# A first batch loaded in parts, unread products in idle stretches, earlier table and statistics, stores in sixteen parts

## The chip, the cores and the metric

The kernel runs on one core of a Trainium2 chip. The metric is the device time of one execution in microseconds; lower is better. A core has five engines that run side by side, each in its own order: TensorE (PE, matrix products), VectorE (DVE), ScalarE (ACT), GpSimd (POOL) and SyncE (SP, which here only issues transfers). They wait for each other by semaphores. Transfers can be issued from SP's, ACT's and POOL's queues.

## What is computed

The input is x with shape (4, 128, 64, 64): four batches of 4096 tokens with 128 channels, in float32. Two layers are run, cut here to what matters.

```python
# layer 0: attention over all 4096 positions of a batch, 64 channels
q, k, v = wq @ xf, wk @ xf, wv @ xf              # xf: (b, 128, 4096)
att = softmax(k^T q, axis=2)                     # (b, 4096, 4096)
x = x + wo @ (att v)
# layer 1
t = tokens(x)                                    # (b, 4096, 128)
t = t + causal_attention(layernorm(t))           # q, k, v by 128x128 weights
wx = batchnorm(layernorm(t) @ W^T)               # mean and variance over all 4*4096 rows
y_0 = 0;  y_s = sigmoid(wx_s + V y_(s-1))        # along the 4096 tokens
out = t + y
```

The batch statistics need every block of every batch, so the recurrence can't begin before the last one.

## The kernel before, in words

All of it is in `fast_path`. A second path, `general_path`, follows in a branch that is taken only if a flag computed at the end asks for it; in the profile it is not taken.

**Opening (L398 to L469, L806 to L821).** The weights are loaded from ACT's queue with `load`, the input from SP's queue in 16 transfers of 512 KB, all four batches one after the other (L410 to L412). PE's first product is `g_ps` (L468), which forms the matrix g1 from wqT and wkT. Then, for batch 0, the function `keys(0, m)` is run for m = 0 to 3, all ahead of the attention: `cols0` makes a block of keys and queries (two products kr_ps, L490, copied by DVE and ACT) and sends half of each copy to other partitions with a transfer (`swap`, L496); `vals0` makes the values (v_ps, L502), and `vals0_by_tokens` transposes them (vT_ps, L512).

**Attention (L693 to L849).** The work of both layers is a list of items. An item scores two tiles of 128 keys against 512 queries (`scores`: s_ps by PE at L704 or L713, an exponential on ACT at L718 or L720); two items later `values` adds up acc on PE (L764 or L772); `sums` adds the exponentials on DVE (L744). Layer 0 takes 16 items for each block of 512 queries; there are eight blocks to a batch. One loop over slots `s` writes this out by hand. In each slot one further piece of work may go in: either one that is due (a block's normalisation, its projection, its LayerNorm) or the next of a list called `side`, which holds the `keys` of the next batch while layer 1 of the present one runs:

```python
            if due:
                w = min(due, key=lambda w: w[0])
                waiting.remove(w)
                w[1]()
                push(s, w[2])
            elif side:
                side.pop(0)()
```

`rows` prepares the queries two blocks ahead, and in layer 0 calls `tokens0`, which overwrites a block of the input in `xs` with the same block laid out by tokens (a transfer from xT, L526).

**A block's end in layer 1 (`finish1`, L618).** Three steps: `first` divides and adds to the residual (`project`), stores the result to x2 and normalises it (`normed`, with a power on POOL at L450); `second` transposes it; `third` multiplies with W (wx_ps, L653), takes batch statistics with bn_stats (L656) into `stats`, and ACT copies wx back into `xs` (L660, L662). For the last block of all (`final`) the transposition is done on PE, as nothing is left to hide a slower way.

**Recurrence and output (L856 to L949).** After the last block, DVE aggregates the 32 statistics (`bn_aggr`, L868), a chain of small operations makes scale and shift, and the recurrence starts. It cuts each batch into 256 chunks that run side by side, 12 warming steps and 16 kept ones, four batches in turn: a product (y_ps, L907), one DVE operation (L909), a sigmoid (L912; the very first at L904). `residual` then transposes the states on PE, adds them on DVE to the residual read back from x2 (L927), and stores each half of a batch, 1 MB, once its 16 steps are done (L928).

The order of instructions on each engine is not wholly the source's: independent instructions may change places when the program is built.

Of the kernel before, what the change touches and what calls it, by code (L numbers as in the profile page):

```python
# [15 lines left out]
P = 128  # L16
# [333 lines left out]
def fast_path(  # L350
# [44 lines left out]

    x2 = dram.tile([B, N, P], F32, name="x2")

    def load(name, shape, *parts):  # L398
        t = const.tile(shape, F32, name=name)
        for dst, src in parts:  # L400
            nc.scalar.dma_start(out=dst(t), in_=src)
# [5 lines left out]
    wqk = load("wqk", [P, P], (lo, c_wqT), (hi, c_wkT))  # L407
    wkq = load("wkq", [P, P], (lo, c_wkT), (hi, c_wqT))
    wv0 = load("wv0", [P, M], (whole, c_wvT))
    for b in range(B):  # L410
        for g in range(N // CHUNK):
            nc.sync.dma_start(out=xs[:, b, ts(g, CHUNK)], in_=x[b, :, ts(g, CHUNK)])  # L412
    wo2 = load("wo2", [P, P], (top, c_woT), (bottom, c_woT))
    wqT = load("wqT", [P, P], (whole, a_wqT))
    wkT = load("wkT", [P, P], (whole, a_wkT))
    wv1 = load("wv1", [P, P], (whole, a_wv))
    wf = load("wf", [P, P], (whole, f_wT))
    vf = load("vf", [P, P], (whole, f_vT))
    gamma = load("gamma", [P, 1], (whole, f_gamma))
    beta = load("beta", [P, 1], (whole, f_beta))  # L420

    ident = const.tile([P, P], F32, name="ident")
    make_identity(nc, ident)
# [16 lines left out]
    quarter = const.tile([P, TPB, Q], F32, name="quarter")  # L440
    for j in range(TPB):
        nc.vector.tensor_reduce(quarter[:, j], ident.rearrange("p (q r) -> p q r", r=S), AX.X, ALU.add)
    good = const.tile([P, 1], F32, name="good")
    g1 = const.tile([P, P], F32, name="g1")
    recs = const.tile([P, 2, B, NT], F32, name="recs")
    stats = const.tile([P, B * NB, nc.vector.BN_STATS_DIM], F32, name="stats")

    def rsqrt(y, var, z):

# [6 lines left out]
    with tc.tile_pool(name="batch", bufs=1) as batch, tc.tile_pool(name="rows", bufs=2) as rowp, tc.tile_pool(  # L456
# [7 lines left out]
        def misc(name):  # L464
            return ps_m.tile([P, BLK], F32, tag="m", name=name)

        gp = misc("g_ps")
        nc.tensor.matmul(gp[:, :P], lhsT=wqT, rhs=wkT, start=True, stop=True)  # L468
        nc.vector.tensor_copy(g1, gp[:, :P])  # L469

        class Batch:
            pass
# [121 lines left out]
        def in_range():  # L594
# [5 lines left out]
            nc.vector.tensor_tensor(r, r, r2, ALU.mult)  # L600
            nc.vector.tensor_reduce(good, r, AX.X, ALU.add)

        def finish0(b, g):

            agg, den = bs[b].agg, bs[b].den

            def norm():
                if g == 0:
                    bs[b].xh = batch.tile([P, NT, P], F32, tag="xh", name="xh")
                    bs[b].xhT = batch.tile([P, N], F32, tag="xhT", name="xhT")  # L610
                normed(b, g, bs[b].xh[:, ts(g, TPB)])

            yield 2, lambda: (project(0, b, g, agg, den), norm())
            fill.append(
                lambda: transposed(bs[b].xh[:, ts(g, TPB)], bs[b].xhT[:, ts(g, BLK)], "xhT_ps", nc.scalar.copy)
            )

        def finish1(b, g):  # L618
            agg, den = bs[b].agg, bs[b].den
            mem = {}  # L620
            final = b == B - 1 and g == NB - 1

            def first():
                project(1, b, g, agg, den)
                nc.sync.dma_start(
                    out=x2[b, ts(g, BLK)].rearrange("(j p) c -> p j c", p=P),
                    in_=xs[:, b, ts(g, BLK)].rearrange("p (j c) -> p j c", c=P),
                )
                mem["xh"] = wk.tile([P, TPB, P], F32, tag="xh2", name="xh2")
                normed(b, g, mem["xh"])  # L630

            def second():
                mem["xhT"] = wk.tile([P, BLK], F32, tag="xhT2", name="xhT2")
                if final:
                    transposed(mem["xh"], mem["xhT"], "xh2T_ps", nc.vector.tensor_copy)
# [13 lines left out]
                nc.sync.dma_start(out=mem["xhT"], in_=by_c.rearrange("c r q k -> (c r) (q k)"))  # L649

            def third():
                wp = misc("wx_ps")
                nc.tensor.matmul(wp, lhsT=wf, rhs=mem["xhT"], start=True, stop=True)  # L653
# [12 lines left out]

            yield 1, first
            yield 3, second
            yield 1 if final else 4, third
# [133 lines left out]
                lambda: vals0_by_tokens(b, m, mem[0]),  # L803
            ]

        for m in range(NB // 2):  # L806
            for task in keys(0, m):
                task()
        SKEW = 2
        side = []  # L810

        def rows():

            if blocks:
                layer, b, g = blocks.pop(0)
                (rows1 if layer else rows0)(b, g)
                if layer == 0:
                    tokens0(b, g)

        rows()  # L820
        rows()  # L821
        for s in range(len(items) + SKEW + 16):
# [8 lines left out]
            if 0 <= s - SKEW < len(items):  # L831
                it = items[s - SKEW]
                values(it)
                if it.last:
                    rows()
                    if fill:
                        fill.pop(0)()
                    push(s, (finish1 if it.layer else finish0)(it.b, it.g))
# [7 lines left out]
                push(s, w[2])  # L846
            elif side:
                side.pop(0)()
        assert not waiting and not side and not fill  # L849


# [4 lines left out]
    with tc.tile_pool(name="xr", bufs=1) as xrp, tc.tile_pool(name="y", bufs=2) as yp, tc.tile_pool(  # L856
# [11 lines left out]
        nc.vector.bn_aggr(mv, stats)  # L868
# [50 lines left out]
        def residual(b):  # L919

            for h in range(HALVES):
                for s0 in range(0, STEPS, TPB):
                    ps = ps_r.tile([P, TPB, P], F32, tag="r", name="yT_ps")
# [86 lines left out]
```

## Time and profile before

| | |
|---|---|
| Time, three runs | 2142.74, 2143.60 (median), 2145.57 us |
| Profiled execution | timed at 2148.17 us, span 2146.4 us |
| PE busy | 2097.3 us (98%) |
| Weight loads of PE (overlap with it) | 922.9 us (43%) |
| DVE, ACT, POOL busy | 1466.3 (68%), 1008.5 (47%), 104.1 us (5%) |
| DMA | 64.99 MB, mean 30 GB/s |

A busy PE means that a product was under way by the records, whose ends are modelled; it does not mean that the array was at its peak. The page also gives the TensorE clock that was granted, in tenths of full speed, for 40 slices of the span. A timeline row has its start, how long it took, engine, line, operation, output and inputs; "x8" merges eight instructions, and the bracket tells how long the engine stood idle before it and what released it. Rows with a small q (SPq, ACTq) issue transfers. All shares are means over stages with different limits, so stages are read one by one.

### The profile page before, as it was taken

To read this page: it belongs to the slowest core of one execution; us is meant where nothing else is said; L and a number is where in the kernel's file an instruction comes from. 1 tells how busy PE (TensorE), PEld (TensorE's weight loads), DVE (VectorE), ACT (ScalarE), POOL (GpSimd) and SP (SyncE) were. 2 spreads that over 40 slices of the span, in tenths; PEclk is the share of its full clock that TensorE was granted. 3 is DMA by queue.
4 is the path that set the end of the run, shared out by engine and by line. 5 is a ranking of instruction groups with operands and counts; after the bars stand their busy time and mean duration, and the time that the engine had idled before them with its cause. 6 is when DMAs were issued, how large, how long until landed. Compare 5 with 4: busy or idle time off the path is not lost. (4 is left out here: it accounts for less than half of the span.)

```text
span 2146.4 us, 30417 instructions
## 1 busy us (share of the span) xinstructions
PE 2097.3 (98%) x12016; PEld 922.9 (43%) x12016; DVE 1466.3 (68%) x2807; ACT 1008.5 (47%) x1098; POOL 104.1 (5%) x207
## 2 busy tenths in 40 slices
PE   6999999999999999999999999999999999999978
PEld 2333344444333344444333334444433334544446
DVE  3788875454788876554588887545478887754478
ACT  3666633323566643333466663332356664323355
POOL 0000010000000000000000001000000001000000
PEclk9999999999999999999999999999999999999989
DMA  7000022000000002110000002200000000110043
GB/s 226 1 1 2 1 60 54 20 15 15 16 2 1 2 6 74 40 30 15 16 1 1 2 1 59 59 16 15 15 16 1 1 2 6 40 30 15 15 162 159
DMA packets 65319, 64.99 MB, mean 30 GB/s; under 512 B 5648, under 2 KB 55056, under 8 KB 63120
## 3 DMA queue, kind: packets, MB, share of 16 engines
q1 hardware_dynamic: 63280, 62.41, 9.7%
q8 instruction: 96, 1.57, 0.3%
q10 hardware_dynamic: 1888, 0.56, 0.1%
q14 instruction: 55, 0.45, 0.1%
HBM read 33.85 MB, written 24.90 MB: 27 GB/s over the span
## 5 line engine op out<-in xcount | busy, mean ns | idle before, releaser
L744 DVE TENSOR_TENSOR dsum<-dsum,p 128x1024 f32<-128x1024 f32 x676 | 826.8, 1223 | 451.6 <-ACT p L720 320.6
L718 ACT ACTIVATE p<-s_ps,nshift 128x1024 f32<-128x1024 f32 x512 | 571.2, 1116 | 356.7 <-PE s_ps L704 337.7
L720 ACT ACTIVATE p<-s_ps 128x1024 f32<-128x1024 f32 (+2 forms) x288 | 274.2, 952 | 564.2 <-PE s_ps L713 542.5
L764 PE MATMUL acc<-p,v 64*64 64x512 f32 x4096 | 533.8, 592 | 1.7 <-ACT half L783 1.7
L704 PE MATMUL s_ps<-swap,kr 64*64 64x512 f32 x2048 | 533.0, 598 | 2.5 <-DMA swap<-kr 2.5
L704 PE MATMUL s_ps<-kr 64*64 64x512 f32 x2048 | 533.0, 598 | 0.0
L713 PE MATMUL s_ps<-rows,xhT 128*128 128x512 f32 (+3 forms) x1152 | 503.1, 559 | 1.4 <-DVE rows L535 1.4
L772 PE MATMUL acc<-p,xh 128*128 128x512 f32 (+3 forms) x1152 | 501.5, 557 | 0.0
L772 PEld LDWEIGHTS acc<-p,xh 128*128 128x128 f32 x1152 | 215.6, 190 | 241.3 <-issue 231.8
L713 PEld LDWEIGHTS s_ps<-rows,xhT 128*128 128x128 f32 x1152 | 212.9, 190 | 242.3 <-issue 196.4
L764 PEld LDWEIGHTS acc<-p,v 64*64 64x64 f32 x4096 | 155.1, 134 | 288.0 <-issue 269.0
L704 PEld LDWEIGHTS s_ps<-swap,kr 64*64 64x64 f32 x2048 | 137.9, 134 | 138.3 <-issue 129.1
L704 PEld LDWEIGHTS s_ps<-kr 64*64 64x64 f32 x2048 | 137.9, 134 | 128.3 <-issue 123.7
L450 POOL TENSOR_TENSOR ln_rstd<-ln_var,mhalf 128x4 f32<-128x4 f32 x64 | 65.7, 1027 | 1211.3 <-DVE ln_var L579 1200.5
L752 DVE TENSOR_TENSOR dsum<-dsum,p 128x256 f32<-128x256 f32 (+1 forms) x120 | 55.7, 498 | 74.3 <-POOL p L724 74.3
L567 DVE SCALAR_TENSOR_TENSOR xs<-o_ps,recs,xs 128x128 f32<-128x128 f32 x256 | 72.3, 343 | 8.7 <-PE o_ps L562 3.1
L583 DVE TENSOR_SCALAR xh<-xs,ln_mv,ln_rstd 128x128 f32<-128x128 f32 x256 | 71.3, 342 | 2.2
L724 POOL TENSOR_SCALAR_AFFINE_SELECT p<-p 128x128 f32<-128x128 f32 x128 | 34.4, 292 | 665.6 <-ACT p L720 650.7
L742 DVE COPY dsum<-p 128x1024 f32<-128x1024 f32 x60 | 41.3, 689 | 35.3 <-ACT p L720 26.6
L576 DVE BATCH_NORM_STATS2 ln_st<-xs 128x6 f32<-128x128 f32 x256 | 63.4, 269 | 0.0
L662 ACT COPY xs<-wx_ps 128x512 f32<-128x512 f32 x31 | 18.1, 585 | 83.6 <-DVE stats L656 76.7
L909 DVE SCALAR_TENSOR_TENSOR z<-xs,scale,y_ps 128x256 f32<-128x256 f32 x108 | 48.5, 480 | 5.7 <-PE y_ps L907 4.4
(115 smaller groups left out, 1043.5 us busy)
## 6 DMA issues: line engine op xcount, KB each, us to landing
xs<-in_x SPq DMA_DIRECT2D x16, 512.0 KB, 8.8
xs<-in_xT SPq DMA_DIRECT2D x32, 256.0 KB, 3.2
x<-xs SPq DMA_DIRECT2D x32, 256.0 KB, 2.3
xr<-x SPq DMA_DIRECT2D x8, 1024.0 KB, 12.3
out_x<-xr SPq DMA_DIRECT2D x8, 1024.0 KB, 6.0
by_c<-sqT SPq DMA_DIRECT2D x124, 64.0 KB, 1.8
xhT<-by_c SPq DMA_DIRECT2D x31, 256.0 KB, 2.7
swap<-kr SPq DMA_DIRECT2D x32, 128.0 KB, 2.2
```

The lines of the kernel that those rows point to most:

```text
L450: nc.gpsimd.tensor_tensor(y, var, mhalf[:, : y.shape[-1]], ALU.pow)
L567: nc.vector.scalar_tensor_tensor(t, in0=op[:, ts(j, P)], scalar=rec[:, j : j + 1], in1=t, op0=ALU.mult, op1=ALU.add)
L576: nc.vector.bn_stats(st[:, j], xs[:, b, ds(g * BLK + j * P, P)])
L583: nc.vector.tensor_scalar(dst[:, j], xs[:, b, ds(g * BLK + j * P, P)], mv[:, j, 0:1], y[:, j : j + 1], ALU.subtract, ALU.mult)
L704: nc.tensor.matmul(ps[c * M : c * M + M, off : off + n], lhsT=bs[it.b].kr[part, h, ds(t % (NT // 2) * P + c * M, M)], rhs=rows[h], start=True,
L713: nc.tensor.matmul(ps[:, off : off + n], lhsT=lhsT, rhs=rhs, start=True, stop=True)
L718: nc.scalar.activation(it.p[:, :off], ps[:, :off], AF.Exp, bias=nshift)
L720: nc.scalar.activation(it.p[:, :off], ps[:, :off], AF.Exp, scale=float(P) ** -0.5)
L744: nc.vector.tensor_tensor(flat, flat, it.p, ALU.add)
L752: nc.vector.tensor_tensor(den[:, h, q0:], den[:, h, q0:], it.p[:, o : o + n], ALU.add)
L764: nc.tensor.matmul(bt.acc[h * M : h * M + M, r], lhsT=bt.v[part, t], rhs=it.p[part, o : o + n], start=it.first, stop=it.last,)
L772: nc.tensor.matmul(bt.acc[:, 0, q0:], lhsT=bt.xh[:, t], rhs=it.p[:, o : o + n], start=it.first and h == 0, stop=it.last and h == 1,)
```

## The change

1. Input: of the input only batch 0 is loaded at the start, in eight transfers of 256 KB, in the order of blocks 0, 4, 1, 5, 2, 6, 3, 7. The next batch is loaded in four transfers of 512 KB while block 0 of the present one ends; a small copy on POOL, which writes into the place to be loaded, makes these transfers wait.
2. Weights: those that the first products don't need go to POOL's queue: wo2, wqT, wkT and wv1 at the start, the others in `load_rest`.
3. `keys(0, m)`: part 0 and the first step of part 1 run ahead of the attention. The rest of part 1, parts 2 and 3, and `form` (g_ps) go to `side`. `tokens0` of the first two blocks is called once `side` is empty.
4. Unread products: twelve of 128 columns before the first keys; in the last block nine, one and six of 256 columns. Their results are not read.
5. Statistics: `ahead` aggregates 31 blocks before the last one and packs count, mean and variance times count into `ends`; the last aggregation has 9 numbers in place of 192.
6. Table: in the last block one sigmoid of one column, read by nobody, stands ahead of `project`.
7. Stores: each half of a batch is stored in two parts of eight steps.

The diff, cut to its core:

```diff
-    for b in range(B):
-        for g in range(N // CHUNK):
-            nc.sync.dma_start(out=xs[:, b, ts(g, CHUNK)], in_=x[b, :, ts(g, CHUNK)])
+    for m in range(NB // 2):
+        for g in (m, m + NB // 2):
+            nc.sync.dma_start(out=xs[:, 0, ts(g, BLK)], in_=x[0, :, ts(g, BLK)])
...
+    wo2 = load(nc.gpsimd, "wo2", [P, P], (top, c_woT), (bottom, c_woT))
+    wqT = load(nc.gpsimd, "wqT", [P, P], (whole, a_wqT))
+    wkT = load(nc.gpsimd, "wkT", [P, P], (whole, a_wkT))
+    wv1 = load(nc.gpsimd, "wv1", [P, P], (whole, a_wv))
...
+    stats = const.tile([P, B * NB - 1, nc.vector.BN_STATS_DIM], F32, name="stats")
+    ends = const.tile([P, 9], F32, name="ends")
+    nc.gpsimd.memset(ends[:, 0:1], float((B * NB - 1) * BLK))
+    spare = const.tile([P, 1], F32, name="spare")
...
+        wp = misc("warm_ps")
+        for _ in range(12):
+            nc.tensor.matmul(wp[:, :P], lhsT=ident, rhs=ident, start=True, stop=True)
+
+        def form():
+            gp = misc("g_ps")
+            nc.tensor.matmul(gp[:, :P], lhsT=wqT, rhs=wkT, start=True, stop=True)
+            nc.vector.tensor_copy(g1, gp[:, :P])
+
+        def load_rest():
+            for t, src in ((wf, f_wT), (vf, f_vT), (gamma, f_gamma), (beta, f_beta)):
+                nc.gpsimd.dma_start(out=t, in_=src)
...
+        def ahead():
+            mv = stat.tile([P, nc.vector.BN_AGGR_DIM], F32, tag="mv1", name="mv1")
+            nc.vector.bn_aggr(mv, stats)
+            nc.vector.tensor_copy(ends[:, 1:2], mv[:, 0:1])
+            nc.vector.tensor_tensor(ends[:, 2:3], mv[:, 1:2], ends[:, 0:1], ALU.mult)
...
             def first():
+                if final:
+                    nc.scalar.activation(spare, agg[:, 0:1], AF.Sigmoid)
                 project(1, b, g, agg, den)
+                if final:
+                    warm(9, agg[:, : BLK // 2])
...
                     transposed(mem["xh"], mem["xhT"], "xh2T_ps", nc.vector.tensor_copy)
+                    warm(1, mem["xh"][:, 2:])
...
-                nc.vector.bn_stats(stats[:, b * NB + g], wp)
+                nc.vector.bn_stats(ends[:, 3:] if final else stats[:, b * NB + g], wp)
+                if b == B - 1 and g == NB - 2:
+                    ahead()
...
                     nc.scalar.copy(to.rearrange("p (s c) -> p s c", c=CPB), wp.rearrange("p (c s) -> p s c", s=STEPS))
+                    warm(6, to[:, : BLK // 2])
...
-        for m in range(NB // 2):
-            for task in keys(0, m):
-                task()
+        parts = [keys(0, m) for m in range(NB // 2)]
+        for task in parts[0][:2] + parts[1][:1] + parts[0][2:]:
+            task()
         SKEW = 2
-        side = []
+        side = parts[1][1:] + parts[2] + parts[3] + [form]
...
+        def tokens():
+            while started:
+                b, g = started.pop(0)
+                tokens0(b, g)
+                if g == 2 and b + 1 < B:
+                    nc.gpsimd.tensor_copy(
+                        xs[:, b + 1].rearrange("p (k n) -> p k n", n=CHUNK)[:, :, 0], bs[b].agg[:, : N // CHUNK]
+                    )
+                    for k in range(N // CHUNK):
+                        nc.sync.dma_start(out=xs[:, b + 1, ts(k, CHUNK)], in_=x[b + 1, :, ts(k, CHUNK)])
...
             elif side:
                 side.pop(0)()
+                if not side and items[s].b == 0 and items[s].layer == 0:
+                    tokens()
+                    load_rest()
...
-        nc.vector.bn_aggr(mv, stats)
+        nc.vector.bn_aggr(mv, ends)
...
-                nc.sync.dma_start(out=by_chunk(out)[b, h], in_=xr[:, b, h])
+                    if s0 % (2 * TPB):
+                        nc.sync.dma_start(out=by_chunk(out)[b, h, :, part], in_=xr[:, b, h, part])
```

More of the change, by code (lines that the diff above doesn't have):

```diff
@@ L396, in fast_path, with load @@
     x2 = dram.tile([B, N, P], F32, name="x2")
-    def load(name, shape, *parts):
+    def load(engine, name, shape, *parts):
         t = const.tile(shape, F32, name=name)
         for dst, src in parts:
-            nc.scalar.dma_start(out=dst(t), in_=src)
+            engine.dma_start(out=dst(t), in_=src)
         return t
@@ L406, in fast_path @@
     top, bottom = (lambda t: t[0:M]), (lambda t: t[M:P])
-    wqk = load("wqk", [P, P], (lo, c_wqT), (hi, c_wkT))
-    wkq = load("wkq", [P, P], (lo, c_wkT), (hi, c_wqT))
-    wv0 = load("wv0", [P, M], (whole, c_wvT))
-    for b in range(B):
-        for g in range(N // CHUNK):
[L412 to L420, printed above, removed]
+    wqk = load(nc.scalar, "wqk", [P, P], (lo, c_wqT), (hi, c_wkT))
+    wkq = load(nc.scalar, "wkq", [P, P], (lo, c_wkT), (hi, c_wqT))
+    wv0 = load(nc.scalar, "wv0", [P, M], (whole, c_wvT))
+    for m in range(NB // 2):
+        for g in (m, m + NB // 2):
+            nc.sync.dma_start(out=xs[:, 0, ts(g, BLK)], in_=x[0, :, ts(g, BLK)])
     ident = const.tile([P, P], F32, name="ident")
@@ L442, in fast_path @@
         nc.vector.tensor_reduce(quarter[:, j], ident.rearrange("p (q r) -> p q r", r=S), AX.X, ALU.add)
+    wf = const.tile([P, P], F32, name="wf")
+    vf = const.tile([P, P], F32, name="vf")
+    gamma = const.tile([P, 1], F32, name="gamma")
+    beta = const.tile([P, 1], F32, name="beta")
+    wo2 = load(nc.gpsimd, "wo2", [P, P], (top, c_woT), (bottom, c_woT))
+    wqT = load(nc.gpsimd, "wqT", [P, P], (whole, a_wqT))
+    wkT = load(nc.gpsimd, "wkT", [P, P], (whole, a_wkT))
+    wv1 = load(nc.gpsimd, "wv1", [P, P], (whole, a_wv))
     good = const.tile([P, 1], F32, name="good")
@@ L445, in fast_path @@
     recs = const.tile([P, 2, B, NT], F32, name="recs")
-    stats = const.tile([P, B * NB, nc.vector.BN_STATS_DIM], F32, name="stats")
+    stats = const.tile([P, B * NB - 1, nc.vector.BN_STATS_DIM], F32, name="stats")
+    ends = const.tile([P, 9], F32, name="ends")
+    nc.gpsimd.memset(ends[:, 0:1], float((B * NB - 1) * BLK))
+    spare = const.tile([P, 1], F32, name="spare")
     def rsqrt(y, var, z):
@@ L465, in misc @@
             return ps_m.tile([P, BLK], F32, tag="m", name=name)
-        gp = misc("g_ps")
-        nc.tensor.matmul(gp[:, :P], lhsT=wqT, rhs=wkT, start=True, stop=True)
-        nc.vector.tensor_copy(g1, gp[:, :P])
+        wp = misc("warm_ps")
[8 more added lines that the diff above has]
+                nc.gpsimd.dma_start(out=t, in_=src)
         class Batch:
@@ L621, in finish1, with warm @@
             final = b == B - 1 and g == NB - 1
+            def warm(n, rhs):
+                ps = ps_s.tile([P, 2 * BLK], F32, tag="s", name="warm_ps")
+                for _ in range(n):
+                    nc.tensor.matmul(ps[:, : BLK // 2].rearrange("p (a c) -> p a c", c=P) if len(rhs.shape) == 3 else ps[:, : BLK // 2], lhsT=ident, rhs=rhs, start=True, stop=True)
             def first():
+                if final:
+                    nc.scalar.activation(spare, agg[:, 0:1], AF.Sigmoid)
                 project(1, b, g, agg, den)
+                if final:
+                    warm(9, agg[:, : BLK // 2])
                 nc.sync.dma_start(
@@ L817, in rows @@
                 if layer == 0:
-                    tokens0(b, g)
+                    started.append((b, g))
+        def tokens():
[8 more added lines that the diff above has]
+                        nc.sync.dma_start(out=xs[:, b + 1, ts(k, CHUNK)], in_=x[b + 1, :, ts(k, CHUNK)])
+        started = []
         rows()
@@ L848, in fast_path @@
                 side.pop(0)()
+                if not side and items[s].b == 0 and items[s].layer == 0:
+                    tokens()
+                    load_rest()
         assert not waiting and not side and not fill
@@ L922, in residual @@
                 for s0 in range(0, STEPS, TPB):
+                    part = slice(s0 - TPB, s0 + TPB)
                     ps = ps_r.tile([P, TPB, P], F32, tag="r", name="yT_ps")
```

## The prediction, made before the changed kernel was run

> **What bounds the kernel now.** I read the page first, then the timeline of the opening and of the end, then the windows (busy time by stretch). The page:
>
> ```profile
> PE 2097.3 (98%) x12016; PEld 922.9 (43%) x12016; DVE 1466.3 (68%) x2807; ACT 1008.5 (47%) x1098; POOL 104.1 (5%) x207
> PEclk9999999999999999999999999999999999999989
> ```
>
> PE is busy for 98% of the span, and from 40 to 2043 us it has no hole that counts (1993.7 of 2003 us busy). The change leaves that stretch's products as they are, so what it is worth lies before 50 us and after 2049 us. The timeline of the opening:
>
> ```profile
> 0.81 20.49 SPq L412 DMA_DIRECT2D xs<-in_x  x16
> 11.79 0.76 PE L468 MATMUL g_ps<-wkT,wqT 128*128 128x128 f32 x2 [11.79 <-DMA wkT<-in_a_wkT]
> 22.30 11.24 SPq L496 DMA_DIRECT2D swap<-kr  x8
> 33.33 1.11 PE L704 MATMUL s_ps<-swap,kr 64*64 64x512 f32 x2 [2.51 <-DMA swap<-kr]
> 38.50 1.40 PE L764 MATMUL acc<-p,v 64*64 64x512 f32 x8
> 49.17 1.03 PE L764 MATMUL acc<-p,v 64*64 64x512 f32 x8
> ```
>
> PE's first instruction, g_ps, waits until 11.79 for a weight late in ACT's queue. Sixteen loads (8 MB) stand ahead of the swap transfers in SP's queue, so the first score starts at 33.33. The seventh value set (acc) starts at 49.17; its end, 50.0, is my mark for comparing. The timeline of the end:
>
> ```profile
> 2058.63 2.08 PE L653 MATMUL wx_ps<-xhT,wf 128*128 128x512 f32 x2 [0.78 <-DVE xhT L592]
> 2061.48 1.02 DVE L868 BATCH_NORM_AGGREGATE mv<-stats 128x2 f32<-128x192 f32 x1
> 2064.89 1.28 ACT L904 ACT_TABLE_LOAD   x1 [2.82 <-DVE shift L876]
> 2066.18 2.07 ACT L904 ACTIVATE y<-xs,shift,scale 128x256 f32<-128x256 f32 x4
> 2068.61 0.51 ACT L912 ACTIVATE y<-z,shift 128x256 f32<-128x256 f32 x1 [0.35 <-DVE z L909]
> ```
>
> This is one serial chain: product, statistics, sum of statistics, table, first sigmoids. After it the recurrence runs at 1.81 us a step (four sigmoids of 0.45 us). The windows (PE, PEld, DVE, ACT and POOL busy, then granted clock, DMA share, GB/s):
>
> ```profile
> 33.30:38.50 5.20, 5.17 (x25) 1.49 (x29) 0.97 (x2) 2.23 (x2) 0.00 (x0) 0.50 0.79 228
> 2053.20:2070.00 16.80, 6.39 (x14) 3.77 (x15) 8.10 (x32) 4.96 (x8) 1.66 (x3) 0.50 0.54 206
> 2122.00:2138.00 16.00, 14.47 (x112) 12.22 (x109) 16.00 (x30) 1.43 (x6) 0.00 (x0) 1.00 1.01 415
> 2138.00:2142.00 4.00, 0.00 (x0) 0.00 (x0) 0.15 (x1) 0.00 (x0) 0.00 (x0) 0.55 1.02 410
> ```
>
> PE runs at half clock in the first scores and all through the chain of the end. From 2122 to 2142 the DMA engines are full with the stores, which outlast DVE's last addition (2138.15).
>
> **What the Trainium skill says.** "TensorE: Matmul & The Clock Gate", Part 1: the clock halves after an idle window of about 3.4 us, and is whole after a busy one; the windows run freely. The trace agrees: PE's recurrence begins at 2066.83 at half clock and is whole at about 2070.2, and a 512-column record took 1061 ns against 592. "DMA: Bandwidth & Descriptors", Specifications: a first byte takes about 1 us when GpSimd issues, 0.6 us from SP or ACT, and the ceiling is 435 GB/s. No GpSimd transfer is in this trace; the ceiling fits 410 to 415. "ScalarE: Activation LUTs", What ACT_TABLE_LOAD costs: 1283 ns and a drain of 1380. The trace has 1.28 us and no drain, as ACT was idle; I use the trace.
>
> **The opening.** Removed: g_ps at PE's head, twelve of sixteen loads from SP's first stretch, nine weight transfers from ACT's queue. ACT then frees at about 3.2 us instead of 11.8, and loads its table there. Added: twelve unread 128-column products at PE's head, and nine transfers and a memset on POOL.
>
> When is PE free for the keys? ident was complete at 1.43; one GpSimd transfer now stands before its last step, so about 2.4 with the skill's 1 us as an estimate. The twelve products are 24 records; g_ps's two began 0.31 apart at half clock, and o_ps's eight (L562, 1.14 us) about 0.12 at full clock. At half clock I take 0.25, so 6.0 us if the clock never rises, 4.6 if it rises at the earliest (3.4 us after they start). PE is free at 7.0 to 8.4; I take 7.8. The data are there: wv0 landed at 7.3 before (issue 2.70, 4.6 to land) with far more traffic, and a first load took 4.2 to 5.3 us from 0.81.
>
> From there to the first score: two key products, v, two of the next part, one transposition. At full clock a 512-column record costs 0.43 (score sets stand 0.857 apart), so 0.86 x 5 + 0.43 = 4.7, with 0.5 for waits on copies, 5.2. The swap path is shorter: product and copy 1.75 (18.00 to 19.75), issue 0.46, landing 2.2, 4.4. First score at 13.0, against 33.33.
>
> From there to the mark, PE has nine score sets and seven value sets, 16 x 0.857 = 13.7. Between them now stand three v (2.6), four key products (3.4), three transpositions (1.3) and g_ps (0.2), 7.5. For the waits that each slot's copy on ACT makes I add 0.8. ACT is not the limit: per four slots 4 x 1.11 + 3 x 0.58 = 6.2 against 10 on PE; nor is DVE, 4 x 1.23 + 0.69. The mark falls at 13.0 + 13.7 + 7.5 + 0.8 = 35.0. **Gain 50.0 - 35.0 = 15.0 us.** Bounds: 17 (PE free at 6.5, swap early) and 11 (ident at 4, or 3.4 us of the scores still at half clock).
>
> **The middle: nothing.** The 12 later loads (2 MB per batch) wait for a small POOL copy, and that for agg, which DVE finishes before the LayerNorm powers that stand behind it on POOL. They are issued on SP when all eight xT loads of that batch (L526) have gone; behind them come transfers only needed some 190 us later, and 2 MB take 5 us at 410 GB/s. wo2 is first read at 70 us, wv1 and the feed-forward weights later. The sum of 31 statistics (1.0 us) and two small operations lie on DVE at about 2029, where it idles 2.21 us before each addition L744. The early sigmoid lies in ACT's idle 11.28 us before L660.
>
> **The end.** On the chain: the four transpositions at full clock 0.2; wx at 1.02 (its rows at 2027) instead of 2.08, 1.05; the sum over 9 numbers at 0.16 (L577) instead of 1.02, 0.86; the table 1.28. Together 3.4. The nine unread products (9 x 0.43 = 3.9) lie between o_ps, done at 2051.4, and the transpositions at 2056.7, and the tenth beside DVE's copy of 0.69. The last six (2.6 at full clock) start with ACT's copy at about 61.0 on the old scale and end at 63.6, when the first state is ready at 63.5. Then the first rounds run at full clock: round three began at 71.5, 5.3 after the first, where two steady rounds take 3.6; worth up to 1.5. But PE idles at 55.3 to 56.7 and 59.4 to 61.0, and only some 40% of 57.6 to 61.0 is busy; before, a window with about 45% (2049.7 to 2053.1) lost the clock. If it is lost, the six take about 4.3 to 5.2 and cost 1.0. I take +0.6 from between. **Gain 4.0**, bounds 2.4 and 4.9.
>
> **The stores.** DVE needs 0.60 us per addition (14.43 / 24), so a store of eight steps is ready 1.2 us before one of sixteen. The DMA engines are full from first to last, so the end moves with the first: **1.2**, bounds 0 (the smaller stores cost it back) and 2.5 (the last half megabyte drains sooner too). Eight more issues of 0.33 fit into SP's gaps.
>
> Sum: 15.0 + 4.0 + 1.2 = 20.2 us. Against its own span 2146.4 this gives 2126.2. That execution was timed at 2148.2, the runs shown at 2142.7 to 2145.6, so from their median 2143.6 I predict **2123.4 us**. A measurement here tells about 0.2% (4 us) from no change.
>
> **Rivals.** (1) The opening gives less: each of nine pieces between the scores waits its turn behind a 1.11 us exponential on ACT, and PE stands 0.8 us each time, 7 more: 2130.5. For it: ACT's order puts every copy behind an exponential. Against: PE has two other sets to do meanwhile. 12%. (2) Slower: those holes keep the clock at half from the first score to the end of the pieces. Its place is 13 to 35 us; PE's 21.2 us of work there would double and eat 21.2 of the 20.2: 2144.6, and slower by over 0.2% once the holes last into the second block (3 us more, 2148). [...]before, 18 to 22 with 3.29 of 4 us kept the full clock, so it is unlikely: 3%, and 1% for landing within 0.2%. (3) The unread products do not hold the clock, as with a free window they may not: the end gives 2.4 and the opening 12, 2128; this lies within my forecast's range. Forecast with it: 84%.
>
> **Range.** Low: 17 + 4.9 + 2.5 saved, 2119.2. High: 11 + 2.4 + 0 saved would be 2130.2; rival 1's 2130.5 is taken in. Faster 0.96, within 0.2% 0.01, slower 0.03.
>
> **What would show it.** First score at about 13 us, seventh value set ended at about 35 and at full clock; POOL's transfers not delaying ident beyond 3; table load at about 2050; wx at about 1.0 us; first sigmoids some 3.4 earlier against the last value set; first store 1.2 earlier, GB/s still above 400. Wrong if the first score stands after 17, if the window 13 to 35 shows a clock near 0.5, or if the stretch between has grown.

## The result and the profile after

| | before | after |
|---|---|---|
| Time, median of four runs | 2144.12 us (2142.74 to 2145.57) | 2129.29 us (2126.45 to 2130.85) |
| Ratio | | 0.9929 [0.9912, 0.9946] |
| Profiled execution: timed, span | 2148.17, 2146.4 us | 2127.96, 2126.2 us |

The change saves 14.8 us between the medians and 20.2 us between the two profiled executions. Most of the gap between these two numbers lies in before: its profiled execution took 4.05 us longer than its median, and after's took 1.33 us less than its own (20.2 - 4.05 - 1.33 = 14.8). The experiments ask what that luck was.

From the page of after:

```profile
PE 2102.6 (99%) x12072; PEld 931.3 (44%) x12072; DVE 1467.1 (69%) x2810; ACT 1009.4 (47%) x1099; POOL 110.2 (5%) x220
PEclk9999999999999999999999999999999999999999
```

PE has 56 more instructions, the unread products, and 5.3 us more busy time in a shorter span. The last slice but one of the clock, 8 before, is 9. The timeline of after's opening (start, length, engine, line, operation, count, and in brackets the idle time before it):

```profile
0.82 5.97 SPq L413 DMA_DIRECT2D xs<-in_x  x8
1.43 0.71 POOL L401 DMA_DIRECT2D wo<-in_c_woT  x1 [0.31 <-issue]
2.61 5.49 PE L475 MATMUL warm_ps<-ident 128*128 128x128 f32 x24 [2.61 <-POOL ident masks.py:199]
7.89 1.11 PE L505 MATMUL kr_ps<-xs,wqk 128*128 128x512 f32 x2
9.76 0.52 SPq L511 DMA_DIRECT2D swap<-kr  x1
13.29 0.65 PE L741 MATMUL s_ps<-swap,kr 64*64 64x512 f32 x2
17.84 1.04 PE L801 MATMUL acc<-p,v 64*64 64x512 f32 x8
36.12 1.04 PE L801 MATMUL acc<-p,v 64*64 64x512 f32 x8
```

The first score stands at 13.29 instead of 33.33. The last row is the seventh value set, which started at 49.17 before: 13.05 us gained by then. The start of this set is called the mark below. The timeline of after's end:

```profile
2035.57 1.28 ACT L654 ACT_TABLE_LOAD   x1
2036.60 4.05 PE L649 MATMUL warm_ps<-agg,ident 128*128 128x256 f32 x18
2043.84 1.13 PE L687 MATMUL wx_ps<-xhT,wf 128*128 128x512 f32 x2 [0.35 <-DVE xhT L607]
2045.73 0.20 DVE L923 BATCH_NORM_AGGREGATE mv<-ends 128x2 f32<-128x9 f32 x1
2046.37 2.86 PE L649 MATMUL warm_ps<-xs,ident 128*128 128x256 f32 x12 [1.41 <-ACT xs L696]
2048.34 2.08 ACT L959 ACTIVATE y<-xs,shift,scale 128x256 f32<-128x256 f32 x4 [2.02 <-DVE shift L931]
```

The table load has left the chain, wx takes 1.13 instead of 2.08 and the aggregation 0.20 instead of 1.02. The windows of after (stretch, its length, then busy time of PE, PEld, DVE, ACT and POOL, granted clock, DMA share, GB/s):

```profile
13.30:36.10 22.80, 22.80 (x153) 7.06 (x156) 10.29 (x10) 14.09 (x18) 0.00 (x0) 1.00 0.42 119
2035.00:2050.50 15.50, 12.01 (x54) 8.84 (x55) 9.14 (x42) 4.71 (x8) 1.66 (x3) 1.00 0.35 120
2103.00:2119.00 16.00, 14.43 (x111) 12.17 (x109) 16.00 (x30) 1.43 (x6) 0.00 (x0) 1.00 1.02 416
2119.00:2122.00 3.00, 0.00 (x0) 0.00 (x0) 0.08 (x1) 0.00 (x0) 0.00 (x0) 0.82 0.98 384
```

From the first score to the seventh value set PE has no hole, and the clock is whole. It is whole through the last block too. The stores still fill the DMA engines at 416 GB/s and still outlast DVE.

Cut at four marks, the two traces give this budget. It is the ledger for every run below.

| stretch (us) | before | after | gained |
|---|---|---|---|
| opening: to the start of the seventh value set | 49.17 | 36.12 | 13.05 |
| middle: to ACT's copy of the last block's value sum (agg) | 2000.44 | 1998.85 | 1.59 |
| end: to the end of DVE's last addition | 88.53 | 84.11 | 4.42 |
| stores: to the end of the span | 8.26 | 7.12 | 1.14 |
| sum | | | 20.20 |

The middle should not have moved: the change leaves its products alone.

### The profile page after: what moved, and what is told of

The parts are those of the page before. It is cut to its first block, busy times and chain, and to the rows that moved or that the text cites. A ratio compares the mean times of both kernels' runs of the same rounds, so it can differ in the third digit from the quotient of the medians.

```text
span 2126.2 us, 30582 instructions
## 1 busy us (share of the span) xinstructions
PE 2102.6 (99%) x12072; PEld 931.3 (44%) x12072; DVE 1467.1 (69%) x2810; ACT 1009.4 (47%) x1099; POOL 110.2 (5%) x220
```

## The experiments

Two theories stood at the start. **A**: the gain is what the budget says, from the opening and the end, and its parts can be taken away one by one. **B**: part of the difference, in either direction, is not the change's but an accident of PE's clock in one execution. Four kernels ran on one chip, four on a second and four on a third, each beside runs of the kernel before on the same chip. Medians and ratios are of these runs; where stretches are compared, they come from one trace each.

**The same kernel again, and the pieces of the change**

`again` is the changed kernel, not edited.

> The changed kernel once more, for more of its runs and a second trace. My theory: the change itself is worth 18.0 us (opening 12.5, end 4.4, stores 1.1); the other 2.2 us between the two profiles are the granted clock at three waits for the product wx in the first scores of batches 1 to 3, which goes to half or not by where its free window falls. So the opening (first score at 13.3, seventh value set at 36.1), the end and the stores repeat within 0.5 us, while the stretch between differs by up to 4 us from run to run. Rival: the change itself has shortened the stretch between by 2.2 us; then that repeats too. Time 2124 to 2132.

`no_unread` takes all 28 unread products away.

```diff
-        for _ in range(12):
-            nc.tensor.matmul(wp[:, :P], lhsT=ident, rhs=ident, start=True, stop=True)
-                    warm(9, agg[:, : BLK // 2])
-                    warm(1, mem["xh"][:, 2:])
-                    warm(6, to[:, : BLK // 2])
```

> All unread products taken out (12 at the head, 9, 1 and 6 in the last block). Theory that they carry the clock: first key product at about 7 us but at half clock, so the first score at 14 to 16 and the first scores at half clock in part; wx back at 2.1 us, the first rounds of the recurrence late by 1.2 us: 3 to 6 us slower than the changed kernel, 2130 to 2134. Rival: they cost PE as much as they give, since the first keys wait for the twelve until 8.1 us: within 1.5 us of the changed kernel.

`open_only` keeps the new opening alone, with its twelve unread products; statistics, table, stores and the end's products are as before.

```diff
-                    nc.scalar.activation(spare, agg[:, 0:1], AF.Sigmoid)
-                    warm(9, agg[:, : BLK // 2])
-                    warm(1, mem["xh"][:, 2:])
-                    warm(6, to[:, : BLK // 2])
-                bn_stats(ends[:, 3:] if final else stats[:, b * NB + g], wp)
+                bn_stats(stats[:, b * NB + g], wp)
-                    ahead()
-        nc.vector.bn_aggr(mv, ends)
+        nc.vector.bn_aggr(mv, stats)
-                    if s0 % (2 * TPB):
-                        dma_start(out=by_chunk(out)[b, h, :, part], in_=xr[:, b, h, part])
+                dma_start(out=by_chunk(out)[b, h], in_=xr[:, b, h])
```

> The opening alone: loads, weights, keys between the scores and the twelve products at the head as changed; the last block, the statistics, the table and the stores as before. By the profiles the end and the stores are worth 4.4 and 1.1, so it should be 5.5 us slower than the changed kernel and 12.5 us faster than before: 2131 to 2135. Rival: the end's gain hangs on something else (the smaller stores cost it back, the clock is lost there anyway): within 2 us of the changed kernel.

`keys_ahead` puts all keys of batch 0 ahead of the attention again, as before did, with the new loads.

```diff
-        for task in parts[0][:2] + parts[1][:1] + parts[0][2:]:
+        for task in parts[0] + parts[1] + parts[2] + parts[3]:
             task()
-        side = parts[1][1:] + parts[2] + parts[3] + [form]
+        side = [form]
```

> As changed, but all sixteen key and value pieces of batch 0 run ahead of the scores as before, so that only the loads, the weights' queue and the twelve products differ there. If the early loads give most: 4.2 us a part from 7.9, first score at about 25, seventh value set at about 39 against 36.1, so 3 us slower than the changed kernel, 2129 to 2134. If the interleaving carries the gain: first score past 30, 8 to 12 us slower. If the interleaved pieces cost PE more than they save (each took 0.15 to 0.4 us more than its bare products): no slower.

Before on this chip: 2144.88 us.

| run | median us | ratio to before | 7th value set | middle | end | stores |
|---|---|---|---|---|---|---|
| again | 2128.19 | 0.9924 [0.9910, 0.9937] | 39.23 | 1997.09 | 84.13 | 7.25 |
| no_unread | 2131.09 | 0.9944 [0.9931, 0.9958] | 37.67 | 1995.21 | 87.49 | 7.13 |
| open_only | 2130.83 | 0.9938 [0.9924, 0.9951] | 36.65 | 1995.38 | 89.12 | 7.95 |
| keys_ahead | 2132.65 | 0.9935 [0.9921, 0.9949] | 43.76 | 1996.97 | 84.14 | 7.23 |

`again` is the surprise. Its time and its end repeat, but its opening does not: the mark falls 3.1 us later than in the first trace of the very same kernel. PE's timeline of `again` shows why:

```profile
11.51 0.66 PE L527 MATMUL vT_ps<-ident,vT 128*128 128x128 f32 x4
14.81 0.65 PE L741 MATMUL s_ps<-swap,kr 64*64 64x512 f32 x2 [2.65 <-DMA swap<-kr]
15.83 1.98 PE L517 MATMUL v_ps<-xs,wv 128*64 128x512 f32 x4
17.73 1.12 PE L741 MATMUL s_ps<-swap,kr 64*64 64x512 f32 x2
20.95 1.04 PE L801 MATMUL acc<-p,v 64*64 64x512 f32 x8
```

PE reached its keys at 6.78 instead of 7.89 and was ready for the first score 1.1 us sooner. But the score needs the swap, and that transfer, issued at 8.56, landed only at 14.8, behind 2 MB of input loads that ran until about 14 us. PE waited 2.65 us, and soon after it the clock was halved: the v set at 15.83 took 1.98 us where after's took 1.08. So the first score is bound by the swap behind the loads once PE is early. `no_unread` says the same from the other side: without the twelve products PE starts its keys at 5.81, and the first score still stands at 13.27, after a wait of 0.96 us for the swap.

`keys_ahead` did not come out as intended. The program's order has the first score ahead of the keys of parts 1 to 3 on PE, and PE stood before it with all that work behind it:

```profile
8.65 1.08 PE L517 MATMUL v_ps<-xs,wv 128*64 128x512 f32 x4
14.03 1.96 PE L741 MATMUL s_ps<-swap,kr 64*64 64x512 f32 x2 [4.30 <-DMA swap<-kr]
16.83 1.91 PE L505 MATMUL kr_ps<-xs,wqk 128*128 128x512 f32 x2
```

It shows that a 4.3 us hole costs its own length and then a half-clock stretch, here from 12.5 to 19.3 us. It is no clean test of keys ahead against keys in `side`. Its five executions fall into two groups: 2128.2 and 2128.6 us at a mean granted clock of 0.999, and 2132.7 to 2133.9 us at 0.996 or 0.997. The trace is of the second group.

`open_only` loses 5.0 us of `again`'s end and 0.7 of its stores, as the budget asks. In time it stands only 2.6 us behind it (2130.83 against 2128.19): its trace had no loss in the middle and a mark 2.6 us earlier. In this table the last two columns repeat to 0.2 us wherever the code is the same; the two before them do not. `no_unread` came out in the range expected of it. Its trace is that of the fastest of its five executions: its end is 3.4 us longer than `again`'s, but its opening and its middle had the better luck.

**What moves the middle.** In the six traces so far the middle is 1995.2 to 1995.4 us, or 1.8, 1.9, 3.6 or 5.2 us more. The places can be found: the third step of block 7, in each of the first three batches, runs four slots after the transposition through DRAM was issued, and there four slots are too short. wx waits for its input to come back. PE's waits between 500 and 1700 us (what waited, for what, us in total, times, longest), first in before and then in after:

```profile
PE wx_ps L653 <- DMA xhT<-by_c: 6.3, 3, 2.3
```

```profile
PE wx_ps L687 <- DMA xhT<-by_c: 5.6, 3, 1.9
```

The windows around these three waits, in before:

```profile
557.00:562.00 5.00, 4.66 (x22) 1.48 (x26) 2.73 (x4) 1.70 (x2) 0.00 (x0) 0.66 0.00 0
1065.00:1070.00 5.00, 3.90 (x14) 1.10 (x18) 3.17 (x4) 0.66 (x2) 0.00 (x0) 0.67 0.08 29
1573.00:1578.50 5.50, 4.01 (x18) 1.23 (x22) 3.58 (x4) 1.23 (x2) 0.00 (x0) 0.70 0.12 45
```

In after:

```profile
544.00:549.00 5.00, 4.15 (x34) 1.47 (x38) 3.13 (x4) 1.71 (x3) 0.00 (x0) 1.00 0.05 17
1051.00:1056.00 5.00, 4.45 (x18) 1.34 (x22) 2.96 (x4) 1.70 (x2) 0.00 (x0) 0.66 0.02 4
1559.00:1564.50 5.50, 4.71 (x22) 1.57 (x26) 3.62 (x5) 1.60 (x2) 0.00 (x0) 0.69 0.03 12
```

And in `again`:

```profile
547.00:552.00 5.00, 4.16 (x34) 1.42 (x34) 3.15 (x4) 1.61 (x3) 0.00 (x0) 1.00 0.07 25
1053.00:1058.00 5.00, 3.48 (x26) 1.27 (x30) 3.68 (x4) 1.08 (x2) 0.00 (x0) 1.00 0.15 51
1560.00:1566.00 6.00, 4.82 (x22) 1.47 (x26) 3.77 (x5) 1.70 (x2) 0.00 (x0) 0.72 0.08 30
```

The clock column is the reading. A mean of 0.66 to 0.72 over five to six microseconds is about 3.4 us at half speed. Before lost it at all three waits, after at two, `again` and `keys_ahead` at one, `no_unread` and `open_only` at none: 1.7 to 1.9 us each time. The same kernel lost it twice in one execution and once in another.

The traces also show when a wait costs the clock. In each of the fourteen traces of this document the changes of the granted clock lie whole multiples of 3.41 us apart, and each loss in the middle is one such step. So the clock goes by windows of 3.41 us, and their place against the program differs from one execution to the next. These are the two windows at before's first wait, then the two at after's:

```profile
554.65:558.07 3.42, 1.51 (x10) 0.30 (x2) 3.11 (x4) 1.10 (x1) 0.00 (x0) 1.00 0.30 77
558.07:561.48 3.41, 3.41 (x17) 1.03 (x20) 1.64 (x2) 1.34 (x2) 0.00 (x0) 0.50 0.00 0
540.54:543.95 3.41, 2.42 (x24) 0.61 (x16) 3.20 (x3) 2.15 (x2) 0.00 (x0) 1.00 0.38 94
543.95:547.36 3.41, 2.51 (x18) 0.95 (x22) 3.10 (x4) 0.07 (x1) 0.00 (x0) 1.00 0.09 29
```

Both waits are of 1.9 us. Before's lies in one window: PE is busy for 1.51 of 3.42 us, and the next window is at half clock. After's is split between two, each with over 2.4 us busy, and nothing is lost. In all the windows of the fourteen traces, half clock followed every window with PE busy for at most 43%, and none with 51% or more; of eleven windows between 44 and 48%, it followed five. (PE's ends are modelled, so these shares are not exact.) The clock went from half to full after windows with 86% or more, PE's first ones included, and after none with 77% or less. Seven traces have the waits at wx, 21 places in all: where the wait lay in one window, to within 0.05 us, the clock was lost in 8 of 13 places, and where it was split, in none of 8.

This agrees with the Trainium skill, "TensorE: Matmul & The Clock Gate", Part 1, which says that the windows over which the clock is decided run freely. The rule of that page's section "HAM oscillation", no idle gap over some 3.4 us, is not strict enough here: these waits are of 1.8 to 2.3 us. To see what the waits cost in all, the wait itself was removed.

**Without the waits at wx, and the swap ahead of the loads**

`wx_later` is the changed kernel with the third step of those blocks two slots later; `before_wx_later` is the kernel before with the same edit.

```diff
-            yield 1 if final else 4, third
+            yield 1 if final else 6 if g == NB - 1 else 4, third
```

> As changed, but the product wx of each batch's last block stands two slots later (for batches 1 to 3's first scores), so that its transfer has landed. Theory: the three waits of 1.8 to 1.9 us there, and the clock lost at some of them (1.7 us each), make the stretch between seventh value set and last agg 1995.2 us plus 1.7 for each loss (before 3 losses, changed 2, its repetition 1). Without the waits it is about 1989.5 with no loss in any trace, and the time falls by 5.5 to 9 us to some 2120, with less spread. Rival, that the stretch varies for another reason (transfers of the next batch, PE's records): it still varies by some us, and the time falls by the waits alone, or less.

> The kernel before with the same two slots more. By the theory it gains what the changed kernel gains or a little more, as its trace had all three losses: 2134 to 2138, and the difference to the changed kernel with the later product is then the change's own worth without the clock's chance: 16 to 18 us. By the rival that the change itself shortens the middle stretch, the difference stays 20.

`swap_first` is the changed kernel with only the first two parts of the input loaded at once. The other two parts follow after the first keys; a small copy on POOL, which reads the first block of keys, holds each of them back.

```diff
-    for m in range(NB // 2):
+    for m in range(2):
         for g in (m, m + NB // 2):
             nc.sync.dma_start(out=xs[:, 0, ts(g, BLK)], in_=x[0, :, ts(g, BLK)])
...
-        for task in parts[0][:2] + parts[1][:1] + parts[0][2:]:
+        parts[0][0]()
+        for m in range(2, NB // 2):
+            for g in (m, m + NB // 2):
+                nc.gpsimd.tensor_copy(xs[:, 0, ds(g * BLK, 1)], bs[0].kr[:, 0, 0:1])
+                nc.sync.dma_start(out=xs[:, 0, ts(g, BLK)], in_=x[0, :, ts(g, BLK)])
+        for task in parts[0][1:2] + parts[1][:1] + parts[0][2:]:
             task()
```

> As changed, but of batch 0 only the four blocks of parts 0 and 1 are loaded at once; the other four wait (by a small copy on POOL) for the first keys, so that the first swap transfer is not behind them. Theory: the first score waits for the swap behind 2 MB of loads, 13.3 to 14.8 us, and in the worse case the wait costs the clock as well (score at 14.81, seventh value set at 39.23, against 13.29 and 36.12). Then here: first score at 12 to 12.6 whenever the first keys start by 7, seventh value set at 34.8 to 35.6 at full clock, 2 to 3 us faster than the repetition. Rival, that the twelve products and the keys' round trips set the first score: no change. A loss is possible if parts 2 and 3 land late: their products then wait at about 18 us.

`both` has the edits of `swap_first` and `wx_later` together.

> Both together: the sum of the two gains if the theory holds, some 8 to 11 us under the changed kernel, 2117 to 2120, and faster than both kernels.

Before on this chip: 2144.01 us.

| run | median us (range) | ratio to before | 7th value set | middle | end | stores |
|---|---|---|---|---|---|---|
| wx_later | 2121.19 (2120.82 to 2124.03) | 0.9894 [0.9877, 0.9911] | 36.05 | 1992.07 | 84.07 | 7.11 |
| before_wx_later | 2137.19 (2135.98 to 2138.48) | 0.9965 [0.9952, 0.9977] | 45.91 | 1991.83 | 89.64 | 8.32 |
| swap_first | 2125.16 (2124.24 to 2127.93) | 0.9913 [0.9897, 0.9928] | 35.05 | 1997.23 | 84.08 | 7.14 |
| both | 2120.90 (2120.04 to 2121.43) | 0.9889 [0.9872, 0.9905] | 35.58 | 1992.06 | 84.06 | 7.30 |

PE's waits in the same stretch of `wx_later` begin with this row, and wx is not among them:

```profile
PE s_ps L741 <- ACT p L755: 1.6, 3, 0.6
```

With the wait gone the middle is 1991.8 to 1992.1 us in three traces out of three, in the kernel before as in the changed one, and no clock is lost there. That is 3.2 us below the best middle with the waits, `no_unread`'s, and 8.6 below that of before's profile. The three waits sum to 5.4 in `no_unread`; 1.6 come back as the new wait on ACT, which the expected 1989.5 had not counted, and some 0.6 of the rest I can't place. One execution of `wx_later` without a trace took 2124.03 us at a mean clock of 0.997, the other three 2120.8 to 2121.4 at 0.999; what it lost, and where, is not known.

Every execution has its mean granted clock on record, traced or not, and the time goes with it. The four of after took 2126.45, 2127.96, 2130.62 and 2130.85 us at 0.998, 0.997, 0.996 and 0.995. Of the 26 of before beside the experiments, the three at 0.990 or 0.991 took 2147.9 to 2148.8 us, and the rest, at 0.992 to 0.994, 2142.3 to 2146.4. One window at half clock is 0.0008 of this mean and 1.7 us of the time.

Three readings follow. First, theory B holds for the middle: what the two first traces differ by there belongs to neither kernel. With 1.7 us taken off for each loss, the middles of the seven traces that have the waits (`swap_first` lost the clock once) agree to 0.3 us. Second, freed of it, the change itself is worth 2137.19 - 2121.19 = 16.0 us, measured on one chip; by stretches of the two traces 9.9 in the opening, -0.2 in the middle, 5.6 in the end and 1.2 in the stores. Before's opening varies as well: its first score to first value set took 5.2 us at half clock in the first profile and 3.3 us at full clock in `before_wx_later`, so part of the 13.05 was luck of the same kind. Third, an edit of one line gains as much again as the end did: on this chip `both` beats `swap_first` by 4.3 us and `before_wx_later` beats before by 6.8, and in neither pair do the runs overlap.

`swap_first` does bring the first score to 12.22 and the mark to 35.05, with no wait as in `again`. Whether that is worth anything in time is not settled: with the waits gone as well, `both` and `wx_later` are level (2120.90 and 2121.19), where 2117 to 2120 was expected of `both`.

**The unread products and the stores, one at a time, from `both`**

`both_no_head` leaves the twelve products at the start out.

```diff
-        for _ in range(12):
-            nc.tensor.matmul(wp[:, :P], lhsT=ident, rhs=ident, start=True, stop=True)
```

> The kernel called both (changed, with the product wx later and the loads of parts 2 and 3 behind the first swap), without the twelve products at the head. If they carry the clock into the scores: first keys at about 5.8 but at half clock, first score at about 12 as before since keys and swap run slower, scores at half clock until about 15: seventh value set 1 to 2.5 us later than with them (35.1 to 35.6), 2122 to 2123.5. If they only delay the keys, now that no load stands before the swap: 1 us faster, under 2120.

`both_no_tail` leaves the sixteen products of the last block out.

```diff
-                    warm(9, agg[:, : BLK // 2])
-                    warm(1, mem["xh"][:, 2:])
-                    warm(6, to[:, : BLK // 2])
```

> As both, without the nine, one and six products in the last block. By the traces without any unread products (last agg to last addition 87.5 us against 84.1) they are worth 3.4 us: 2124 to 2125. The prediction had 1.25 of the 3.4 for wx and transposition and +0.6 for the first rounds, 1.9 in all: 2122.8.

`both_stores_8` stores whole halves again.

```diff
-                    if s0 % (2 * TPB):
-                        dma_start(out=by_chunk(out)[b, h, :, part], in_=xr[:, b, h, part])
+                dma_start(out=by_chunk(out)[b, h], in_=xr[:, b, h])
```

> As both, with the stores whole again (eight of 1 MB). From the last addition to the end 8.0 to 8.3 us in place of 7.1: 0.8 to 1.2 us slower, 2121.8 to 2122.2. If the gain came from elsewhere: the same time.

`both_stores_32` stores after every addition, four steps at a time.

```diff
-                    if s0 % (2 * TPB):
-                        dma_start(out=by_chunk(out)[b, h, :, part], in_=xr[:, b, h, part])
+                    dma_start(out=by_chunk(out)[b, h, :, ds(s0, TPB)], in_=t)
```

> As both, with stores of four steps (32 of 256 KB, 2 KB a row). If the end follows the first store: 0.6 us earlier still, 2120.3. If DVE's additions bound the end by now (0.60 us for 256 KB, 437 GB/s, above what the DMA engines moved, 380 to 415), or if smaller rows cost: no gain or a loss of up to 1 us.

Before on this chip: 2144.93 us; the middle is 1992.0 to 1992.1 in all four.

| run | median us (range) | ratio to before | 7th value set | end | stores |
|---|---|---|---|---|---|
| both_no_head | 2123.97 (2123.13 to 2124.90) | 0.9905 [0.9888, 0.9921] | 36.44 | 85.79 | 7.1 |
| both_no_tail | 2123.76 (2123.28 to 2124.78) | 0.9904 [0.9887, 0.9920] | 34.94 | 87.02 | 7.5 |
| both_stores_8 | 2122.03 (2120.74 to 2122.36) | 0.9893 [0.9876, 0.9909] | 36.30 | 84.14 | 7.8 |
| both_stores_32 | 2121.18 (2120.09 to 2121.52) | 0.9889 [0.9873, 0.9906] | 36.17 | 84.08 | 7.0 |

Without the tail's products the last block runs at half clock. The windows of `both_no_tail`, from just after the last value sum into the recurrence, whose first sigmoids start at 2041.47:

```profile
2028.00:2034.00 6.00, 0.79 (x8) 0.60 (x6) 4.60 (x24) 1.08 (x2) 1.01 (x1) 0.92 0.15 44
2034.00:2041.00 7.00, 3.23 (x6) 1.23 (x6) 3.39 (x14) 0.58 (x1) 0.65 (x2) 0.50 0.21 70
2041.00:2046.00 5.00, 3.88 (x9) 3.16 (x10) 1.70 (x6) 3.49 (x7) 0.00 (x0) 0.50 1.02 428
```

PE is busy 0.79 of 6 us, and the clock goes to 0.50 at 2033.1 and stays there through the chain's products into the recurrence. After's windows over this stretch, shown above, have 12.01 of 15.5 us busy and a clock of 1.00. The time says 2.9 us (against `both` on another chip; the ratios are 0.9904 and 0.9889, with intervals that overlap; of the two kernels of this chip that have all the products and differ in the stores alone, no execution took more than 2122.36 us, and of this one none less than 2123.28). The traces say 3.0, below the 3.4 expected and above the 1.9 of the prediction: the chain (from ACT's copy of agg to the first sigmoids) 14.47 instead of 13.36, from the first sigmoids to the last of the warming steps 22.17 instead of 20.36.

Without the products at the head the first keys run at half clock, as PE's timeline of `both_no_head` shows:

```profile
5.36 2.05 PE L502 MATMUL kr_ps<-xs,wqk 128*128 128x512 f32 x2 [5.36 <-DMA wqk<-in_c_wkT]
7.20 1.91 PE L502 MATMUL kr_ps<-xs,wkq 128*128 128x512 f32 x2
12.03 1.07 PE L738 MATMUL s_ps<-swap,kr 64*64 64x512 f32 x2
13.61 0.64 PE L738 MATMUL s_ps<-swap,kr 64*64 64x512 f32 x1
13.62 0.65 PE L738 MATMUL s_ps<-kr 64*64 64x512 f32 x2
```

They start 2.1 us sooner than in `both`, but from there to the v set at 9.05 they need 3.69 us, where after needed 1.90. The first score starts 0.7 us sooner than in `both`, and yet the mark falls 0.9 us later. That is not the clock, which is whole from 9.2 us on. Without the twelve products the program was built in another order: the first score set runs in two pieces, two records at 12.03 and the other six from 13.61 on. In `both` all eight run side by side:

```profile
12.75 0.65 PE L741 MATMUL s_ps<-swap,kr 64*64 64x512 f32 x2
12.77 0.65 PE L741 MATMUL s_ps<-kr 64*64 64x512 f32 x2
```

The extra piece takes 1.0 us; without it the two marks would be within 0.2 us of each other. So what the twelve products gain by the clock, and what they cost by keeping PE from its keys, about cancel here (the v set starts at 9.05 against 9.25 in `both`), and the run does not show that they are worth anything. In time it is slower than both kernels of this chip with all the products (2123.13 to 2124.90 against 2120.09 to 2122.36 us). In its trace 0.9 us of that is the mark, and 1.7 us are a half-clock stretch in the last block (2040.1 to 2043.6), where its products are those of `both`; the window before it had PE busy for 48%. So the tail's products don't hold the clock for certain; they make it likely: it was held in eight of the nine traces that have them, and in none of the five that don't.

Of the stores, whole halves cost 0.5 us by the trace and 1.1 by the time, 32 parts gain nothing. Both lie within the intervals of `both`.

## Why the prediction was right and where it was wrong

It forecast faster, and the range holds the result; the stated 2123.4 us is 5.9 below the measured 2129.3. The sum made against the profile's own span, 20.2 us and a span of 2126.2, equals the measured pair, but the terms do not: opening 2.0 too much, middle 1.6 too little, end 0.4 too little, stores 0.1 too much. That they cancel is chance.

- **The step that failed is the subtraction**: "That execution was timed at 2148.2, the runs shown at 2142.7 to 2145.6, so from their median 2143.6 I predict 2123.4". A gain worked out against one execution was taken from the median of others. That the execution stood 4 to 5 us above the median was said and not asked about. Its mean clock was 0.990, that of the executions of before near their median 0.992 or 0.993: some two to four windows at half clock, 1.7 us each. Its trace shows five such windows, three at wx and two under the first scores. A loss that the median run has only in part can't be gained in full.
- **"The middle: nothing"** is right of the change: with the waits gone, the middles of both kernels agree to 0.3 us. What I misread was the page's row of nines and "no hole that counts". In 2000 us three holes of about 2 us are 0.3%, and they do count, since each can cost 1.7 us beyond itself.
- **The opening, 15.0**: 13.05 in the first pair, 9.9 in the pair without waits. Its mark of before was in part chance: the set stood at 49.17 there and at 45.91 in `before_wx_later`, whose opening is the same code. PE free at 7.8 (measured 7.89, 6.78 in `again`) and first score at 13.0 (13.29) were right where PE was late. The 6.78 lies below the stated 7.0 to 8.4: the clock was whole 2.9 us after the first of the twelve products there (2.61 to 5.54) and 5.5 us after it in the first trace, where the prediction had 3.4 us as the earliest. The mis-sized term is "7.5 + 0.8" for the pieces between the score sets: from the first score to the end of the seventh value set 23.7 us were measured, where 22.0 were predicted (the 0.2 for g_ps in it came after the mark). v took 1.01 us instead of 0.86, a pair of keys 1.91 instead of 1.72, a transposition 0.59 instead of 0.43; that is 1.3 us in the sum, and the sets beside a piece took 0.91 to 1.02 instead of 0.857, 1.4 more. PE has no idle time there. Products of other shapes alternate in this stretch, which I take for the cause; no run tested it.
- **"Landing 2.2, 4.4"** for the swap was too short a path where PE is early: 6.2 us from issue to landing in `again`, behind the 2 MB of loads, and 2.3 in `swap_first` without half of them. It set the first score at 14.8 there and with it a clock loss.
- **The end, 3.4 and 0.6**: the chain gave 3.20, the first rounds 1.22; in the pair without waits the end gave 5.6, as the half clock of `before_wx_later` reached 2.4 us further into the rounds than before's. The clock held through the last block in after, so the rounds gave what stood as "up to 1.5". The products of the tail are worth about 2.9 together, where the prediction's own terms (0.2 + 1.05 + 0.6) make 1.9. Statistics and table were not tested alone; `no_unread`, which keeps them, has a chain of 14.47 against 16.57 before, 2.10 for 0.86 + 1.28.
- **The stores, 1.2**: 1.14 in the pair, 0.5 to 1.1 in the run that undoes them.
- **The rivals.** Rival 1 (pieces that cost more) was right in kind, for 2 of its 7 us, though not by its mechanism: PE does not stand, its products take longer. Rival 2, half clock from 13 to 35 us, did not come; `again` had some 3 us of it. Rival 3, products that don't hold the clock, was not seen in after, and once in `both_no_head`.

What stays open: whether the swap ahead of the loads gains anything in time, the value of keys in `side` against keys ahead, whether the twelve products at the head gain anything, and what decides on the clock where a window is busy for 44 to 48%.

The best version tried is the changed kernel with wx two slots later in the last block of each batch, with or without the swap first: 2121 us, 0.9894 [0.9877, 0.9911] and 0.9889 [0.9872, 0.9905] of before.

## What to carry to other kernels

Before a gain worked out in one profile is taken from a median, ask what that execution lost by chance, and leave those losses out of both sides. A busy share of 98% doesn't rule out holes that matter: list the waits of the busiest engine by size, as each one of about 2 us can also cost a half-clock stretch. Whether it does changes from one execution to the next, so a difference of a few such stretches between two traces is not yet the change's; the mean clock of each execution tells. Moving the waiting product two slots later bought here as much as the whole new end. Where a run takes instructions out, compare the order on the engine before a difference is put down to what went. Where a small transfer feeds the first product, look at what stands in the queue ahead of it before making the engine that waits for it faster.

## What was not expected of the hardware

- A wait of PE of 1.8 to 2.3 us cost 1.7 us more in 8 of 21 places in seven traces (3 in before, 2 in after, 1 each in `again`, `keys_ahead` and `swap_first`), and nothing in the others; the place in the program was the same. It was lost only where the wait lay within one of the clock's windows of 3.41 us, so that PE was busy for less than half of it. A wait of 2.65 us cost the clock too. After's last block, with idle stretches of up to 1.4 us, kept it.
- Issuing a transfer from GpSimd took 0.71 us the first time and 0.55 to 0.63 us each time after. Nine issues kept POOL until 6.9 us, and the identity that the first products needed was done at 2.56 instead of 1.43 (the prediction had about 2.4).
